# Layer 2 of a four-layer convolution kernel: who stores its sums, when squares are taken, and where raw strips are scaled

## Chip, core and metric

The kernel runs on one core of one Trainium2 chip, in float32 throughout. Times are microseconds (us) on the device. PE stands for TensorE's matmuls, PEld for its weight loads, DVE for VectorE, ACT for ScalarE, POOL for GpSimd and SP for SyncE, which here only issues DMAs. ScalarE and GpSimd have DMA queues of their own too, and issue from them in order with their other instructions.

## The reference

A tensor `x` of 4 images, 384 channels and 64x64 pixels goes through four layers, each of the form `x = x + layer(groupnorm(x))`: attention on 96 channels with a projection (layer 0), a patchwise Fourier filter with a gated depthwise convolution (layer 1), the block below (layer 2), and a 7x7 depthwise convolution whose kernels depend on the data (layer 3). The change lies in layer 2 and at the end of layer 1. Layer 2 begins so (`_bn` normalises each channel over the whole batch):

```python
kw = jax.nn.softmax(_bn(_pw(a, kp_w2), kp_g2, kp_b2), axis=1)
y3 = _bn(_dw(x, c3_w, 1), c3_g, c3_b)
y5 = _bn(_dw(x, c5_w, 2), c5_g, c5_b)
y1 = x * c1_w.reshape(1, -1, 1, 1) + c1_b.reshape(1, -1, 1, 1)
tok = _bn(kw[:, 0:1] * y3 + kw[:, 1:2] * y5 + y1, ar_g, ar_b)
```

`tok` is then gated and goes through a two-layer channel network. The statistics of `tok` over the batch (its sum and sum of squares by channel) are needed before that network can start.

## The kernel before

**End of layer 1.** `layer1` works on bands of eight image rows. `band_out` (L1142) multiplies a band's 512 pixels with the output weights, three output blocks `o` of 128 channels with two matmuls each, adds the block to `x` on VectorE, and stores the result to `x1`. For the last image it also calls `raw_strips` after the first block: four TensorE transposes of the first 128 channels, copied by ScalarE into `z`, the array of strips that layer 2's convolution reads. These strips are raw, since the group norm of the last image isn't known yet. The first blocks of the other images come normalised.

**Layer 2's first stage, `phase_b` (L1200).** It runs over twelve units of 32 channels for all four images. `strip_factors` makes scale and shift of the last image's strips by channel, spread over partitions (one matmul with `mean128`), and `scale_strips` applies them with a multiplication and an addition on VectorE, 32 channels at a time: the first quarter before the convolutions, the others in unit 0 after steps 3, 7 and 11.

A unit has sixteen steps `n`, one for a pair of channels. `matrices53` builds the banded matrix `toep` of a pair, by VectorE and GpSimd in turn (from the fifth on, odd ones by GpSimd), some three steps ahead; GpSimd's queue also loads the taps, once in four steps. `conv53` runs the 3x3 and 5x5 convolutions of the pair as matmuls into a PSUM bank `conv_m` (four banks), ScalarE copies it out to `d_o` in two copies, VectorE takes its statistics, and after each fourth step ScalarE's queue stores 1 MB to `d53`. When the unit's steps are done, `conv_norms` turns its statistics into coefficients `s` and `s0`.

**The sums of a unit, `unit_tok` (L1476).** A unit later, the results are read back in another layout, in four loads of 1 MB on SP's queue (`load_results`, pool `b_c` of three buffers), and combined with the normalised input in `unit_x`. Each quarter has two halves `h`: ScalarE writes the product of input and `c1_w` into a PSUM bank `tok_m` (one bank; for the last unit the four of `conv_m`), and two VectorE instructions add the two convolutions, the second writing over `unit_x` and summing up. After the second half ScalarE squares the quarter (writing into the spent `c_d`, for the sum of squares only), and SP's queue stores it to `tok`. It is a generator: each `yield` ends a piece, and `phase_b` takes a piece at even steps from 2 on and at step 15 (in the last unit after nearly every step).

**The strips of the next unit, `unit_strips` (L1301).** Loads of `unit_x` on SP's queue (two tiles of 2048 columns, eight DMAs each), norms on ScalarE by 1024 columns, and, from the fifth unit on, transposes on TensorE with copies by ScalarE and VectorE into `z`. A unit's strips begin at step 11 of the unit two before. The pool `b_x` has six tiles; a tile comes free when its two stores to `tok` have landed.

`units` turns the norm into the layout of units, and `nets` is the small network of `kw` and a gate, in three pieces taken at every third step. `tok_stats` ends the stage, and the channel network's matmuls (L1649) follow in `phase_ef`.

The framework orders instructions of each engine at build time by priority (mostly the order in the program) and by when it reckons that they are ready, and puts in the semaphores. So engines run their instructions in a fixed order, which need not be that of the text. PSUM has eight banks: four for `conv_m`, one for `band7_p`, two for small products, one for `tok_m`.

## Time and profile before

| what | us |
|---|---|
| median of three runs | 4839.67 (4834.68 to 4847.07) |
| profiled execution | 4846.3 |
| its span, first to last instruction | 4844.5 |
| first convolution of layer 2 starts | 2458.29 |
| last convolution of layer 2 ends | 3023.8 |
| first matmul of the channel network | 3069.84 |
| stores of `tok`, issued on SP | 48 of 0.34 |
| squares on ScalarE (L1501) | 48 of 1.15, and 0.19 to read the sum |
| products on ScalarE (L1489) | 96 of 0.78 |
| `scale_strips` on VectorE (L1183, L1184) | 8 of 1.95 to 2.05 |

The span is what the profile covers; the time of an execution is 1.8 us longer. A row of the waits names the waiting engine and line, what ended the wait, and the total, the number and the longest of such waits. The granted clock of TensorE was 0.951 of full speed in the mean.

### The profile page before, as it was taken

To read this page: it belongs to the slowest core of one execution; us is meant where nothing else is said; L and a number is where in the kernel's file an instruction comes from. 1 tells how busy PE (TensorE), PEld (TensorE's weight loads), DVE (VectorE), ACT (ScalarE), POOL (GpSimd) and SP (SyncE) were. 2 spreads that over 40 slices of the span, in tenths; PEclk is the share of its full clock that TensorE was granted. 3 is DMA by queue.
4 is the path that set the end of the run, shared out by engine and by line. 5 is a ranking of instruction groups with operands and counts; after the bars stand their busy time and mean duration, and the time that the engine had idled before them with its cause. 6 is when DMAs were issued, how large, how long until landed. Compare 5 with 4: busy or idle time off the path is not lost. (4 is left out here: it accounts for less than half of the span.)

```text
span 4844.5 us, 49738 instructions
## 1 busy us (share of the span) xinstructions
PE 4396.7 (91%) x18447; PEld 2451.9 (51%) x18447; DVE 2909.2 (60%) x4654; ACT 1994.1 (41%) x2976; POOL 757.3 (16%) x644
## 2 busy tenths in 40 slices
PE   7999999999999999989977988699999997778888
PEld 2233444344443444435466888344444443667888
DVE  6766555645656455556777777555521113767898
ACT  4444434444444444335345565221233334763321
POOL 1000000000000000000044555000000001235544
PEclk9999999999999999989988989899999998788999
DMA  4312211211112111123258888866654444895776
GB/s 141 104 38 68 74 53 66 73 52 46 65 60 68 40 59 59 52 73 109 72 157 283 299 295 299 282 258 252 239 232 152 156 156 156 325 342 181 231 256 232
DMA packets 289087, 745.55 MB, mean 154 GB/s; under 512 B 22491, under 2 KB 122950, under 8 KB 276806
## 3 DMA queue, kind: packets, MB, share of 16 engines
q1 hardware_dynamic: 226168, 452.52, 29.3%
q0 software_dynamic: 36624, 168.19, 9.2%
q10 hardware_dynamic: 26046, 121.58, 6.3%
q8 instruction: 149, 2.44, 0.2%
q14 instruction: 100, 0.82, 0.1%
HBM read 439.95 MB, written 302.25 MB: 153 GB/s over the span
## 5 line engine op out<-in xcount | busy, mean ns | idle before, releaser
L819 ACT ACTIVATE probs<-sc_s 128x1024 f32<-128x1024 f32 x512 | 496.5, 1019 | 689.2 <-PE av L929 588.2
L929 PE MATMUL av<-probs,vt 128*128 128x512 f32 x1536 | 715.0, 602 | 0.0
L1128 DVE SCALAR_TENSOR_TENSOR acc<-band,vecs,acc 128x512 f32<-128x512 f32 x708 | 494.0, 745 | 49.8 <-POOL band L1089 45.5
L1705 PE MATMUL h_m<-f_h,cm_w_t 128*128 128x512 f32 x1152 | 497.6, 596 | 7.4 <-ACT f_h L1693 7.4
L1411 PE MATMUL conv_m<-toep,z 128*128 128x192 f32 (+1 forms) x2304 | 446.9, 355 | 17.0 <-DVE z L1184 6.2
L929 PEld LDWEIGHTS av<-probs,vt 128*128 128x128 f32 x1536 | 276.3, 191 | 337.5 <-issue 333.8
L1411 PEld LDWEIGHTS conv_m<-toep,z 128*128 128x128 f32 x2304 | 409.0, 197 | 40.1 <-DVE z L1184 6.3
L2019 PE MATMUL conv_m<-toep,z 128*128 128x128 f32 x3072 | 393.7, 286 | 38.4 <-POOL toep L2006 16.9
L2019 PEld LDWEIGHTS conv_m<-toep,z 128*128 128x128 f32 x3072 | 379.7, 203 | 40.4 <-POOL toep L2006 17.3
L1649 PE MATMUL h_s<-e_tok,cm_w_t 128*128 128x512 f32 x768 | 363.1, 596 | 4.1 <-DVE e_tok L1634 4.1
L1705 PEld LDWEIGHTS h_m<-f_h,cm_w_t 128*128 128x128 f32 x1152 | 220.4, 191 | 284.6 <-issue 274.0
L1713 DVE BATCH_NORM_STATS2 h_st<-f_h 128x6 f32<-128x512 f32 x96 | 66.4, 694 | 430.1 <-ACT f_h L1712 430.1
L811 PE MATMUL sc_s<-q,k 32*128 32x512 f32 x2048 | 307.5, 642 | 15.4 <-ACT probs L819 15.2
L1392 POOL TENSOR_TENSOR toep<-w,band 128x1280 f32<-128x1280 f32 x94 | 276.1, 2938 | 240.3 <-PE conv_m L1411 234.8
L1051 PE MATMUL t_m<-w_in_t,xb 128*128 128x384 f32 x768 | 279.9, 500 | 4.7 <-DVE coef L1068 4.7
L965 PE MATMUL proj_m<-xm,w_proj_t 128*128 128x512 f32 x576 | 271.7, 611 | 6.3 <-DVE xm L904 4.9
L1656 ACT COPY e_h<-h_s 128x1024 f32<-128x1024 f32 x96 | 97.2, 1012 | 400.7 <-PE h_s L1649 400.7
L1658 DVE BATCH_NORM_STATS2 h_st<-e_h 128x6 f32<-128x512 f32 x192 | 123.5, 685 | 213.2 <-ACT e_h L1656 213.2
L1649 PEld LDWEIGHTS h_s<-e_tok,cm_w_t 128*128 128x128 f32 x768 | 147.1, 192 | 188.1 <-issue 183.4
L1051 PEld LDWEIGHTS t_m<-w_in_t,xb 128*128 128x128 f32 x768 | 143.2, 193 | 141.7 <-issue 56.1
L972 DVE SCALAR_TENSOR_TENSOR x_res<-proj_m,bn_c,x_res 128x512 f32<-128x512 f32 x96 | 71.7, 747 | 236.5 <-PE proj_m L965 236.3
L1649 PE MATMUL h_s<-z,cm_w_t 128*128 128x512 f32 x384 | 197.1, 595 | 0.0
(433 smaller groups left out, 6417.3 us busy)
## 6 DMA issues: line engine op xcount, KB each, us to landing
d<-d_o ACTq DMA_DIRECT2D x48, 1024.0 KB
c_d<-d SPq DMA_DIRECT2D x48, 1024.0 KB
hid<-e_h ACTq DMA_DIRECT2D x16, 3072.0 KB
f_h<-hid SPq DMA_DIRECT2D x16, 3072.0 KB
x_in<-in_x SPq DMA_DIRECT2D x96, 256.0 KB
x_res<-in_x SPq DMA_DIRECT2D x32, 768.0 KB
xa<-x_res POOLq DMA_DIRECT2D x32, 768.0 KB, 3.9
xa_out<-xa SPq DMA_DIRECT2D x32, 768.0 KB
```

Of the source, the lines that this page charges most:

```text
L811: nc.tensor.matmul(s[:, g], lhsT=k4[32 * g : 32 * g + 32, c], rhs=q[i][32 * g : 32 * g + 32], start=True, stop=True,)
L819: nc.scalar.activation(p[:, h * 1024 : (h + 1) * 1024], s[:, 2 * h : 2 * h + 2].rearrange("p a b -> p (a b)"), AF.Exp, scale=0.25,)
L929: nc.tensor.matmul(av[0], lhsT=vt[:, 4 * c + v, :], rhs=p[:, v * 512 : (v + 1) * 512], start=c == 0 and v == 0, stop=c == 7 and v == 3,)
L965: nc.tensor.matmul(m, lhsT=self.w_proj[:, j, o * P : (o + 1) * P], rhs=xm[:, j], start=j == 0, stop=j == NJ - 1,)
L1051: nc.tensor.matmul(m[:, 0:C], lhsT=xb[:, j], rhs=self.w_in[:, j, :], start=j == 0, stop=j == NJ - 1,)
L1128: nc.vector.scalar_tensor_tensor(out, src(j, k), w, done, ALU.mult, ALU.add)
L1392: eng.tensor_tensor(t, self.w53[:, at : at + 160].rearrange("p (m n) -> p m n", n=8).unsqueeze(2).to_broadcast([P, 20, 8, 8]), band.rearra ...
L1411: nc.tensor.matmul(m[:, c * 256 + to : c * 256 + to + 64 * (k1 - k0)], lhsT=self.z_[:, at : at + P], rhs=t[:, 10 * c + k0 : 10 * c + k1].r ...
L1649: nc.tensor.matmul(s[:, v, :], lhsT=w1[:, j, o * P : (o + 1) * P], rhs=t[j][:, v * 512 : (v + 1) * 512], start=j == 0, stop=j == NJ - 1,)
L1658: nc.vector.bn_stats(st[:, o, 8 * b + 2 * i + v, :], h[:, o, v * 512 : (v + 1) * 512])
L1705: nc.tensor.matmul(m, lhsT=w2[:, o, j * P : (j + 1) * P], rhs=h[:, o, v * 512 : (v + 1) * 512], start=o == 0, stop=o == 5,)
L2019: nc.tensor.matmul(m[:, ch * P : (ch + 1) * P], lhsT=self.z_[:, at : at + P], rhs=t[:, 8 * c + 2 * i : 8 * c + 2 * i + 2].rearrange("p m a ...
```

## The change

In `band_out` the raw strips of the last image are made after all three output blocks. `scale_strips` takes the first channel, a count and an engine: VectorE scales 8 channels after one matrix and 24 more after three, GpSimd scales the other three quarters, at the same steps as before. `units` and the set-up of `nets` move behind the first convolution. At step 0 of a unit three results of the unit before are asked for at once, and the fourth after the first quarter's square. Products have two banks of their own in all units, `conv_m` three. The square and the store of a quarter are made in the next piece, after that piece's product, and the store is issued by ScalarE; the last quarter's square and store of a unit come at step 0 of the unit after the next (`before`).

```diff
--- before.py
+++ after.py
@@ -1150,9 +1150,9 @@
                 m, lhsT=self.w_out[64:P, 1, o * P : (o + 1) * P], rhs=acc[2][64:P], start=False, stop=True
             )
             nc.vector.tensor_add(x[:, o], x[:, o], m)
-            if o == 0 and b == B - 1:
-                self.raw_strips(b, h, x[:, 0])
             yield 2.0
+        if b == B - 1:
+            self.raw_strips(b, h, x[:, 0])
         self.stats(st, x, h)
         nc.gpsimd.dma_start(self.x1[b][:, :, h * 512 : (h + 1) * 512], x)
 
@@ -1175,13 +1175,13 @@
         nc.tensor.matmul(m, lhsT=self.mean128, rhs=t.rearrange("p i c -> p (i c)"), start=True, stop=True)
         nc.vector.tensor_copy(self.z_rep, m.rearrange("p (i c) -> p i c", i=2))
 
-    def scale_strips(self, b, q):
-
-        at = slice(32 * q, 32 * q + 32)
+    def scale_strips(self, b, c0, n, eng):
+
+        at = slice(c0, c0 + n)
         zv = self.z[:, at, 1:33, b]
-        of = lambda i: self.z_rep[:, i, at].unsqueeze(2).to_broadcast([P, 32, 32])
-        self.nc.vector.tensor_mul(zv, zv, of(0))
-        self.nc.vector.tensor_add(zv, zv, of(1))
+        of = lambda i: self.z_rep[:, i, at].unsqueeze(2).to_broadcast([P, n, 32])
+        eng.tensor_mul(zv, zv, of(0))
+        eng.tensor_add(zv, zv, of(1))
 
     def coef(self, name):
         return self.keep.tile([P, NJ, B], F32, tag=name, name=name)
@@ -1216,27 +1216,34 @@
             nc.gpsimd.memset(self.mean128, 1.0 / P)
             self.toep = {}
             for n in range(LEAD + 2):
-                if n == 2:
+                if n == 1:
                     self.strip_factors(B - 1)
-                    self.scale_strips(B - 1, 0)
+                    self.scale_strips(B - 1, 0, 8, nc.vector)
+                if n == 3:
+                    self.scale_strips(B - 1, 8, 24, nc.vector)
                 self.matrices53(n)
-            self.units(cp)
             self.unit_x = [[] for _ in range(UNITS)]
             first, strips, behind = self.unit_strips(0), self.unit_strips(1), None
-            for _ in range(3):
-                next(first)
+            next(first)
             for u in range(UNITS):
                 st = self.bt_p.tile([P, 2, 16, 6], F32, tag="st", name="st")
                 tok = self.unit_tok(u - 1) if u else first
-                nets = iter(()) if u else self.nets(cp)
                 for n in range(16):
                     if u or n > 1:
                         self.matrices53(16 * u + n + LEAD)
                     self.conv53(u, n, st)
+                    if n == 0 and not u:
+                        self.units(cp)
+                        nets = self.nets(cp)
+                        for _ in range(2):
+                            next(first)
+                    if n == 0 and u > 1:
+                        next(before, None)
                     if n == 0 and u:
+                        self.results = [self.load_results(u - 1, i) for i in range(3)]
                         self.conv_norms(u - 1, behind)
                     if not u and n in (3, 7, 11):
-                        self.scale_strips(B - 1, n // 4 + 1)
+                        self.scale_strips(B - 1, 8 * n + 8, 32, nc.gpsimd)
                     if n % 2:
                         next(strips, None)
                     elif n or not u:
@@ -1256,10 +1263,10 @@
                         next(coming)
                         if n == 15:
                             strips = coming
-                behind = st
-            results = [self.load_results(UNITS - 1, i, self.bx_p, "x") for i in range(4)]
+                behind, before = st, tok
+            self.results = [self.load_results(UNITS - 1, i, self.bx_p, "x") for i in range(4)]
             self.conv_norms(UNITS - 1, behind)
-            for _ in self.unit_tok(UNITS - 1, results):
+            for _ in self.unit_tok(UNITS - 1):
                 pass
             self.tok_stats()
         self.taps_s.close()
@@ -1404,7 +1411,7 @@
         t = self.toep.pop(16 * u + n)
         if n % 4 == 0:
             self.d_o = self.bt_p.tile([P, 8, 2, P], F32, tag="d_o", name="d_o")
-        m = self.psum.tile([P, 512], F32, tag="c", name="conv_m", bufs=4)
+        m = self.psum.tile([P, 512], F32, tag="c", name="conv_m", bufs=3)
         for c in range(2):
             for i, k0, k1, to in ((1, 3, 7, 0), (0, 0, 3, 0), (2, 7, 10, 64)):
                 at = (c0 + c) * 132 + 4 * i
@@ -1465,7 +1472,8 @@
         nc.vector.scalar_tensor_tensor(s0, m[:, 7:8], -1.0, s0, ALU.mult, ALU.add)
         self.tok_s = s, s0
 
-    def load_results(self, u, i, pool, tag):
+    def load_results(self, u, i, pool=None, tag="d"):
+        pool = pool or self.bc_p
         d = pool.tile([P, 2 * 8 * P], F32, tag=tag, name="c_d").rearrange("p (y v n) -> p y v n", v=2, n=P)
         self.nc.sync.dma_start(
             d.rearrange("p y v n -> p y (v n)"),
@@ -1473,22 +1481,25 @@
         )
         return d
 
-    def unit_tok(self, u, results=None):
-
-        nc = self.nc
-        j, q = u // 4, u % 4
+    def unit_tok(self, u):
+
+        nc = self.nc
         s, s0 = self.tok_s
+        results, self.results = self.results, None
+        behind = None
         for i in range(4):
-            sl = slice(i * 1024, (i + 1) * 1024)
-            d = results[i] if results else self.load_results(u, i, self.bc_p, "d")
+            d = results[i]
             o = self.unit_x[u][i // 2][:, i % 2 * 1024 : i % 2 * 1024 + 1024]
             for h in range(2):
                 part = slice(h * 512, (h + 1) * 512)
-                last = u == UNITS - 1
-                m = self.psum.tile([P, 512], F32, tag="c" if last else "t", name="tok_m", bufs=4 if last else 1)
+                m = self.psum.tile([P, 512], F32, tag="t", name="tok_m", bufs=2)
                 nc.scalar.activation(
                     m, o[:, part], AF.Identity, bias=s0, scale=self.vec("c1_w")[:, u : u + 1]
                 )
+                if h == 0 and behind is not None:
+                    self.square_and_store(u, *behind)
+                    if len(results) == 3:
+                        results.append(self.load_results(u, 3))
                 mv, ov = (t.rearrange("p (y n) -> p y n", n=P) for t in (m, o[:, part]))
                 of = lambda v: d[:, 4 * h : 4 * h + 4, v]
                 nc.vector.scalar_tensor_tensor(mv, of(1), s[:, 1:2], mv, ALU.mult, ALU.add)
@@ -1496,17 +1507,21 @@
                 nc.vector.scalar_tensor_tensor(
                     ov, of(0), s[:, 0:1], mv, ALU.mult, ALU.add, accum_out=self.total[:, u, k : k + 1]
                 )
-                if h == 0:
-                    yield
-            nc.scalar.activation(
-                d.rearrange("p y v n -> p (y v n)")[:, 0:1024],
-                o,
-                AF.Square,
-                bias=self.about[:, u : u + 1],
-                accum_out=self.squares[:, u, i : i + 1],
-            )
-            nc.sync.dma_start(self.tok[u, :, :, sl].rearrange("b c n -> (b c) n"), o)
-            yield
+                yield
+            behind = i, d, o
+        self.square_and_store(u, *behind)
+
+    def square_and_store(self, u, i, d, o):
+
+        nc = self.nc
+        nc.scalar.activation(
+            d.rearrange("p y v n -> p (y v n)")[:, 0:1024],
+            o,
+            AF.Square,
+            bias=self.about[:, u : u + 1],
+            accum_out=self.squares[:, u, i : i + 1],
+        )
+        nc.scalar.dma_start(self.tok[u, :, :, i * 1024 : i * 1024 + 1024].rearrange("b c n -> (b c) n"), o)
 
     def tok_stats(self):
 
```

## The prediction

> **What bounds the kernel now.** I read the page first, for the stage that the change touches. The engine row says that TensorE is busy nine tenths of the span, and the slices say where it is not: the changed code runs from about 2430 to 3070 us, slices 20 to 25.
>
> ```profile
> PE 4396.7 (91%) x18447; PEld 2451.9 (51%) x18447; DVE 2909.2 (60%) x4654; ACT 1994.1 (41%) x2976; POOL 757.3 (16%) x644
> ...
> PE   7999999999999999989977988699999997778888
> ...
> PEclk9999999999999999989988989899999998788999
> ```
>
> The 7, 7 and 6 among nines are layer 2's convolution stage. Next I cut it at the matmuls of `conv_norms` (L1443), which come once a unit, and asked for busy times in these stretches: unit 0, units 2, 3, 8, 9 and 10, and the tail up to the first matmul of the next stage.
>
> ```profile
> 2458.30:2507.60 49.30, 42.51 (x210) 38.94 (x210) 44.67 (x79) 27.07 (x56) 30.80 (x13) 0.90 0.41 135
> ...
> 2548.00:2584.60 36.60, 36.29 (x204) 34.37 (x204) 34.27 (x72) 23.91 (x56) 25.35 (x13) 1.00 0.89 305
> 2584.60:2654.30 69.70, 38.70 (x211) 35.49 (x211) 43.68 (x88) 38.83 (x76) 23.17 (x12) 0.77 0.83 275
> ...
> 2843.00:2889.30 46.30, 39.39 (x223) 36.66 (x221) 35.85 (x74) 29.36 (x63) 25.58 (x12) 0.91 0.93 319
> 2889.30:2935.30 46.00, 44.18 (x246) 41.62 (x247) 36.34 (x74) 27.94 (x61) 25.57 (x12) 0.94 0.88 284
> 2935.30:2984.50 49.20, 39.45 (x224) 36.73 (x223) 36.75 (x75) 29.45 (x63) 25.57 (x12) 0.88 0.94 323
> ...
> 3024.00:3069.80 45.80, 5.04 (x24) 4.13 (x24) 24.07 (x84) 21.45 (x40) 0.58 (x1) 0.54 0.90 301
> ```
>
> Columns are the stretch, its length, busy PE, PEld, DVE, ACT and POOL, clock, DMA share and GB/s. The reader is to see a stage that reaches TensorE's pace once (unit 2) and loses 6 to 10 us a unit later and 30 us in unit 3, while DMA is nearly full all the time. What ends the idle time stands in the waits from 2480 to 3026 us (total, times, longest):
>
> ```profile
> PEld strip_m L1335 <- ACT unit_x L1320: 58.0, 12, 22.5
> ACT tok_m L1489 <- DVE unit_x L1496: 54.7, 33, 5.6
> ACT c_d L1501 <- DVE unit_x L1496: 23.1, 25, 2.7
> ```
>
> TensorE waits for ScalarE's norm of the next strips; ScalarE is held in order by products that wait for their one bank and squares that wait for VectorE. The norms need loads, so the last view is the waits of the SP queue, 2440 to 3060 us:
>
> ```profile
> SPq L1312 <- DMA d<-d_o: 125.1, 17, 33.1
> SPq L1508 <- DVE st L1425: 101.3, 18, 15.9
> SPq L1312 <- DMA tok<-unit_x: 56.2, 18, 6.4
> SPq L1508 <- DVE unit_x L1496: 48.7, 11, 17.2
> ```
>
> Stores of sums (L1508) stand in SP's queue until VectorE is done (180 us with the smaller rows), with loads behind them. The timeline shows the stage's start, and the chain of waits its tail:
>
> ```profile
> 2456.28 1.96 DVE L1184 TENSOR_TENSOR z<-z,z_rep 128x1024 f32<-128x1024 f32 x1
> ...
> 2458.29 12.47 PE L1411 MATMUL conv_m<-toep,z 128*128 128x256 f32 x60 [6.22 <-DVE z L1184]
> ```
> ```profile
> 3030.86 10.59 DMA tok<-unit_x
> 3041.48 0.05 issue
> 3041.59 8.38 DMA c_d<-d
> ```
>
> **What the Trainium skill says.** *SBUF — State Buffer*, "Who interferes with whom": a VectorE instruction with two SBUF inputs contends with a GpSimd one that reads SBUF, and the later one blocks fully. The trace agrees: a 12x1 product (L385) took 2.10 us and a GpSimd matrix 5.61 instead of 2.9 us while both engines worked on SBUF. *DMA: Bandwidth & Descriptors*, "Issuing engines are not separate DMA queues": the queues of SP and ScalarE end on the same 16 engines, so a second issuer saves only issuing time. Total rate staying at 275 to 325 GB/s with two queues at work doesn't contradict it, and I credit no bandwidth. *TensorE: Matmul & The Clock Gate*, Part 1: an idle array drops to half clock and needs some us of work to come back. Here the twelve matmuls of a pair of channels take 2.2 us in steady running and 4.5 us after a stall, so each stall costs about 2 us more than its length, and strips 1 us more.
>
> **The change part by part**, from the profiled execution's 4846.3 us (span 4844.5, 1.8 around it), which is 6.6 above the median of 4839.7.
>
> *Raw strips behind the outputs.* For the last image's eight bands the four transposes no longer make TensorE wait for VectorE's add between outputs. At the last band the second output's matmul stood at 2436.76 behind transposes from 2435.77; it comes 1 us earlier, and with it the norm. Bands before have TensorE at 19 of 20 us; nothing is taken for them. −1 us, between 0 and −3.
>
> *First scale in 8 channels, fewer matrices ahead.* The norm is known at 2445.7, the first convolution starts at 2458.3: 12.6 us with five matrices (1.44 to 1.48 each), factors, and two passes of 1.96 us on VectorE. Afterwards what must precede it is one matrix 1.4, factors 0.5, their matmul 1.2, copy 0.4, and two passes over 256 instead of 1024 elements, about 0.5 each: 4.5 to 5 us with waits between. That is −7.5, and the 24 further channels (two passes of about 1.5) lie beside the first four pairs at about 2.5 us each. Bounds −4 to −9.
>
> *Three scalings on GpSimd.* Six passes of 1.97 us (11.8) leave VectorE in unit 0, where ScalarE waited 8.08 us for the nets' L385 and TensorE 4.94 us behind it. GpSimd pays. Price: its matrices take 2.9 us for 1280 elements, so 2.3 for 1024; *GPSIMD Engine Reference*, 3.1, gives 4497 ns for 2048, the same. Six are 13.9 us on 30.8 busy in unit 0's 49.3: nearly full, and the tap loads in GpSimd's queue come up to 4.6 us later, covered by the three matrices of lead (6.5 us). The nets' small products can still be locked out for 2.3 us each. −3 us, between −8 and +6.
>
> *Stores on ScalarE's queue.* 48 issues of 0.34 us leave SP; SP's loads stand behind no store. ScalarE pays 1.4 us a unit, of 40 where it is busy 24 to 29: no cost by itself. Each store now waits for its square (1.33 us later than before), which frees `unit_x` for loads later by that. Behind a store on ScalarE stand the evacuations of `conv_m`, and TensorE behind them.
>
> *Two banks for products, squares a piece later, three results at once.* The 77.8 us of ScalarE waiting on VectorE go where a bank is free and the square's data old. In unit 3's catch-up (2630 to 2652) a block of two halves takes 5.98 us in lockstep; VectorE's four passes and reads alone are 3.1 and ScalarE's three steps 2.9. Four blocks in the stall save about 11 us if the lag stays. The lag arose since unit 0's results were asked for only at 2532.3, 25 us after its last convolution, behind sixteen strip loads; asked for first, the stall of 22.13+5.13+2.52 us could go whole. I take −18, between −8 and −28. For the boundaries of units 4 to 10 the idle times before strips, norms and the next convolution add to 34.5 us in the timeline, with slow clock about 50. What is late next is the load of the second half tile, now behind three results of 1 MB: at some 300 GB/s, 3.5 us each, plus 9 us until the last `d` has landed, it comes about 22 us into a unit of 40. Its norm belongs at the seventh pair (15 us). So a third: −17, between −40 and +20.
>
> *Banks of `conv_m` 4 to 3.* TensorE's run-ahead falls from 8.7 to 6.5 us. The longest string of other work on ScalarE is product 0.78, square 1.33, issue 0.34, norm 1.24, two strip copies 1.2: 4.9 us. Nominally free; +5 for pile-ups, between 0 and +20.
>
> *Tail.* Results 3 and 4 waited for unit 10's last store, which stood on SP behind result 1 and landed after 10.59 us beside result 2. On ScalarE's queue it leaves 1 to 2 us earlier and in its own ring. −4, between 0 and −8. Two banks instead of four cost nothing, VectorE (1.5 us a half) sets the pace.
>
> Sum: −1 −7.5 −3 −18 −17 +5 −4 = −45.5: 4801 for an execution like the profiled one, 4794 for the median; I say 4795.
>
> **Rivals.** *DMA is the bound.* For it: share 0.83 to 0.94 in every unit and unchanged bytes. Against it: unit 2 ran at TensorE's pace with 0.89, and 2843 to 2858 us has gaps. Then only the start, the lockstep saving and the tail stay, −20: 4820. *ScalarE's queue blocks (slower).* SP's loads waited 125 us for completions of `d` stores that they don't read, so a DMA is held until an older one of either queue is done. If one of the eight stores a unit that ScalarE now issues is held so, behind loads that wait for buffers, all evacuations stand. It decides from 6.5 us, three banks. The wait at 2962.85 was 10.82 us: 4.3 lost plus 2 for the clock, and the norm behind it as late, say 8 a unit, eleven units: +88; the gains at boundaries and half of unit 3's go (17+9), leaving −20: about +68 at full strength, half the units +24; I put it at 4870. Against it: ScalarE's 48 `d` stores show no such wait longer than 0.8 us. *It doesn't take effect*: the instruction order may hoist loads as before; then 4836.
>
> **How the numbers follow.** Forecast 0.48 (its own range 4765 to 4825), DMA bound 0.24 (a quarter of it within the bound), blocked queue 0.26, no effect 0.02. A measurement of this kernel can tell about 0.3%, 14.5 us. Faster 0.48+0.18 = 0.66, same 0.06+0.02 = 0.08, slower 0.26. The range reaches down to 4750 (all boundary stalls and unit 3's gone) and up to 4868, leaving out about half of the slower case and a few per cent below.
>
> **What would show it.** Right: the first convolution about 5 us after the last image's norm, where it is 12.6 now; unit 3 below 55 us; ScalarE's waits for `unit_x` from VectorE under 25 us; results asked for within 10 us of a unit's last convolution. Wrong: ScalarE idle before `d_o` or a store with DMA as releaser, matmuls waiting for `d_o`, GpSimd's matrices ending waits of TensorE in unit 0, or strips still waiting for `unit_x` loads for more than 30 us.

## The result, and the profile after

The changed kernel takes 4795.86 us (median of four runs, 4790.60 to 4806.85) where the kernel before took 4840.60 beside it: a ratio of 0.991, with a 95% interval of 0.9888 to 0.9932. The forecast was 4795. That the sum came out is half luck, though. Several terms missed, in opposite directions, and the table below says where the time went.

First the page of the changed kernel, the same rows as before: busy times, and the slices of the span.

```profile
PE 4391.7 (92%) x18447; PEld 2441.5 (51%) x18447; DVE 2902.5 (61%) x4650; ACT 1992.9 (42%) x2976; POOL 771.0 (16%) x650
...
PE   7999999999999999989978998799999996778888
...
PEclk9999999999999999999989999899999998788999
```

Over the whole span busy times hardly moved (GpSimd has 14 us more), while the span fell from 4844.5 to 4796.5 us. The stage alone looks different. From the last image's norm to the channel network TensorE's idle time fell from 126.0 to 89.3 us, and its busy time from 498.2 to 483.0 for the same 2710 matmuls, with a granted clock of 0.93 in the mean, 0.87 before. Units 4 to 10 show it best, before and after (columns: stretch, length, busy PE, PEld, DVE, ACT and POOL, clock, DMA share, GB/s):

```profile
2654.30:2984.50 330.20, 295.64 (x1638) 276.57 (x1639) 251.73 (x507) 198.22 (x430) 178.95 (x84) 0.92 0.89 297
2653.60:2945.80 292.20, 277.95 (x1639) 261.09 (x1638) 252.16 (x512) 199.05 (x434) 178.75 (x85) 1.00 0.98 332
```

Of the 38 us, 20.3 are idle time and 17.7 are busy time that a full clock shortened. (Before the norm TensorE was busy 9.1 us longer in the second profile, so that the sums over the span are alike.) The stretches below are again cut at the matmuls of `cn_rep` (now L1450): units 0, 1 and 3, a steady unit (8), and the tail.

```profile
2468.78:2517.91 49.13, 43.28 (x213) 39.95 (x213) 41.67 (x76) 26.91 (x57) 36.69 (x17) 0.90 0.49 166
2517.91:2564.10 46.19, 42.97 (x215) 40.41 (x216) 33.77 (x69) 25.62 (x55) 25.23 (x13) 0.89 0.84 288
2607.00:2653.60 46.60, 40.19 (x223) 37.36 (x224) 36.61 (x74) 29.47 (x65) 23.15 (x12) 0.93 0.92 309
2820.40:2862.08 41.68, 39.69 (x235) 37.30 (x235) 35.98 (x74) 28.66 (x63) 25.56 (x13) 1.00 0.98 333
2981.40:3027.20 45.80, 4.68 (x25) 3.72 (x24) 24.11 (x81) 19.52 (x36) 0.59 (x1) 0.56 0.97 315
```

The reader is to see unit 8: TensorE busy 39.7 of 41.7 us at full clock, at the highest DMA rate of any stretch here. Every unit from the fourth to the tenth now takes 41.7 to 42.0 us, where before they took 44.4 to 50.1. Unit 3 went from 69.7 to 46.6. Unit 1 grew from 40.3 to 46.2, and the tail stayed.

The waits from the start of unit 0 to the last convolution (2480 to 2984 us; total, times, longest):

```profile
ACT unit_x L1327 <- DMA unit_x<-x: 27.1, 12, 8.2
...
ACT c_d L1517 <- DVE unit_x L1507: 19.2, 18, 3.2
...
ACT tok_m L1496 <- DVE unit_x L1507: 6.0, 5, 3.7
```
```profile
PEld conv_m L1418 <- ACT d_o L1429: 15.7, 9, 2.1
...
PEld strip_m L1342 <- ACT unit_x L1327: 4.7, 1, 4.7
```

ScalarE's product no longer waits for VectorE (54.7 before, 6.0 now), and TensorE no longer waits for the strips' norm (58.0, now 4.7). New is the 15.7 us that the weight loads put down to a `conv_m` bank, 4.1 before. In seven of the nine cases, just before a unit's end, the matmul itself names VectorE's copy of the next strips into `z` (L1347), which ended 0.4 us after the bank came free in the one I followed (2817.26 and 2816.85 us). ScalarE waits for input loads 27.1 us, where it was 6.2; that reaches TensorE only once.

**One thing has to be taken out before stages are compared.** The last image's norm (L1028) became known at 2445.67 us in the profile before and at 2454.95 here, and in the twelve further kernels anywhere from 2436.7 to 2453.6. Layer 1 differs among them only in the place of the raw strips, so most of this is drift between executions. The fair measure of the stage is from that norm to the first matmul of the channel network:

| us | before | after | forecast | measured |
|---|---|---|---|---|
| last band's first output matmul to norm | 15.8 | 17.9 | −1 | +2.1 |
| norm to first convolution | 12.6 | 13.8 | −7.5 | +1.2 |
| unit 0 | 49.3 | 49.1 | −3 and +5 | −0.2 |
| units 1 to 3 | 146.6 | 135.7 | −18 | −10.9 |
| units 4 to 10 | 330.3 | 292.2 | −17 | −38.0 |
| unit 11 | 39.2 | 35.6 | none | −3.6 |
| tail | 46.1 | 45.8 | −4 | −0.3 |
| norm to channel network | 624.2 | 572.3 | | −51.9 |

The rows add up to −49.7, beside −45.5 forecast. (What follows the stage took 5.4 us less in the second profile and wasn't touched. What precedes the last band took 7.1 more; there the edit reaches the last image's seven other bands, and it saves 0.7 us in the last two of them, as the section on the raw strips shows.) The last row of a single profile is good to about 5 us: two variants below differ by 5 there and not in time.

### The profile page after: what moved, and what is told of

It is laid out like the page before. It is cut to its first block, busy times and chain, and to the rows that moved or that the text cites. A ratio compares the mean times of both kernels' runs of the same rounds, so it can differ in the third digit from the quotient of the medians.

```text
span 4796.5 us, 49708 instructions
## 1 busy us (share of the span) xinstructions
PE 4391.7 (92%) x18447; PEld 2441.5 (51%) x18447; DVE 2902.5 (61%) x4650; ACT 1992.9 (42%) x2976; POOL 771.0 (16%) x650
## 3 DMA queue, kind: packets, MB, share of 16 engines
q8 instruction: 149, 2.44, 0.2%
## 5 line engine op out<-in xcount | busy, mean ns | idle before, releaser
L1418 PEld LDWEIGHTS conv_m<-toep,z 128*128 128x128 f32 x2304 | 403.6, 195 | 54.2 <-ACT d_o L1429 15.7
```

The source lines that it names most:

```text
L1418: nc.tensor.matmul(m[:, c * 256 + to : c * 256 + to + 64 * (k1 - k0)], lhsT=self.z_[:, at : at + P], rhs=t[:, 10 * c + k0 : 10 * c + k1].r ...
```

## The experiments

All times are medians; ratios are to the kernel before on the same chip. "Stage" is the last row of the table above.

### The start: who scales, and when (e1_scale_dve, e2_scale_behind)

The timeline of the changed kernel's start, by GpSimd, VectorE and TensorE, shows why the first convolution came later rather than earlier:

```profile
2459.72 5.03 POOL L1183 TENSOR_TENSOR z<-z,z_rep 128x1024 f32<-128x1024 f32 x2 [8.86 <-DVE z_rep L1176]
2464.70 6.18 POOL L1184 TENSOR_TENSOR z<-z,z_rep 128x1024 f32<-128x1024 f32 x2
```
```profile
2460.89 5.22 DVE L1183 TENSOR_TENSOR z<-z,z_rep 128x256 f32<-128x256 f32 x2
2465.96 6.33 DVE L1184 TENSOR_TENSOR z<-z,z_rep 128x256 f32<-128x256 f32 x2
```
```profile
2468.78 1.54 PE L1418 MATMUL conv_m<-toep,z 128*128 128x256 f32 x3 [8.84 <-DVE z L1184]
```

GpSimd's scalings stand in the program after steps 3, 7 and 11. Beyond the raw strips they depend on nothing but `z_rep`, and the framework put them at the head of GpSimd's order. So they ran beside VectorE's scalings for the first pairs. (A row of the timeline that joins two instructions shows the shape of the first: each of VectorE's rows is the pass over 8 channels and the pass over 24.) Two kernels take this apart. The first gives the three scalings back to VectorE:

```diff
-                        self.scale_strips(B - 1, 8 * n + 8, 32, nc.gpsimd)
+                        self.scale_strips(B - 1, 8 * n + 8, 32, nc.vector)
```

> The changed kernel with the three later scalings on VectorE instead of GpSimd. In the changed kernel the first convolution starts 13.9 us after the last image's norm is known (2468.8 against 2454.9), where about 5 were forecast. Theory (GpSimd's passes over z were ordered ahead of VectorE's two small ones and hold the shared SBUF port): VectorE's small passes take about 0.5 us each instead of 2.6 to 3.2, the first convolution comes 5 to 7 us after the norm, unit 0 becomes some us longer, and the whole time falls by 2 to 8 us. Rival (the chain of factors, their matmul and the copy is itself so long): the first convolution stays 12 us or more after the norm, and the time doesn't fall.

The second leaves them on GpSimd but orders them behind its matrices:

```diff
-        eng.tensor_mul(zv, zv, of(0))
-        eng.tensor_add(zv, zv, of(1))
+        behind = self.tc.issue_after(self.pool_toep.ins) if eng is self.nc.gpsimd else nullcontext()
+        with behind:
+            eng.tensor_mul(zv, zv, of(0))
+            eng.tensor_add(zv, zv, of(1))
...
+        if eng is nc.gpsimd:
+            self.pool_toep = made
```

> The changed kernel with each GpSimd scaling ordered behind GpSimd's latest matrix. Theory (shared port at the start): first convolution 5 to 7 us after the norm, unit 0 no longer than 49 us up to the first statistics matmul, time about 8 us below the changed kernel (4788). Rival (GpSimd is then too full in unit 0, its matrices come late): TensorE waits for GpSimd's matrices in unit 0 and the gain is given back, time unchanged within 4 us.

VectorE's part of the timeline with GpSimd ordered behind:

```profile
2454.48 2.02 DVE L1185 TENSOR_TENSOR z<-z,z_rep 128x256 f32<-128x256 f32 x2
2456.41 2.04 DVE L1186 TENSOR_TENSOR z<-z,z_rep 128x256 f32<-128x256 f32 x2
```

The same four passes take 4.06 us alone and 11.55 beside GpSimd. That fits the lock of the Trainium skill's *SBUF — State Buffer*, "Who interferes with whom", which the prediction named for the small products of unit 0 and not for the place where it hit. In both kernels the first convolution comes 8.5 us after the norm, not 13.8. It isn't 5, since in the framework's order three matrices and the multiplication of the other 24 channels still stand ahead of it.

Neither kernel is clearly faster, however: 4792.08 us (0.9897, 0.9877 to 0.9917) and 4791.96 (0.9898, 0.9880 to 0.9916). Unit 0 grew to 55.2 and 55.1 us, so that from the norm to the end of unit 0 it took 63.8 and 63.7, with 63.0 in the changed kernel and 62.0 before. So the start's gain is given back within unit 0. With GpSimd ordered behind, TensorE waits there 7.4 us for the unit's last statistics and 2.9 us for a bank, and none of its waits is ended by a GpSimd matrix, which the rival had expected. I read this as a scaling that has to be paid beside unit 0's matrices and nets by one engine or the other; which instruction costs the time isn't shown.

### The raw strips (e7_raw_old)

```diff
+            if o == 0 and b == B - 1:
+                self.raw_strips(b, h, x[:, 0])
             yield 2.0
-        if b == B - 1:
-            self.raw_strips(b, h, x[:, 0])
```

> The changed kernel with the raw strips made after the first output block, as before. The last image's norm is known 17.9 us after the last band's first output matmul in the changed kernel, 15.8 us before the change. Theory A (moving the strips made the end of layer 1 longer, since the array stayed at low clock): 15.8 again, and time 2 us less. Theory B (the clock's state at that place is chance): the length depends on when TensorE comes to full clock, not on the strips' place; 15 to 18 us, time unchanged within 4 us.

The old place gives 4787.47 us (0.9888, 0.9869 to 0.9908), 8 below the changed kernel in separate comparisons. The intervals of the two overlap, and the stage is 571.7 us, the same. What differs in the traces is the end of layer 1. TensorE's timeline of the last band, changed kernel first, then with the old place:

```profile
2441.04 2.07 PE L1148 MATMUL out_m<-acc,w_out_t 128*128 128x512 f32 x2
2443.04 2.07 PE L1149 MATMUL out_m<-acc,w_out_t 64*128 64x512 f32 x2
2445.04 2.07 PE L1148 MATMUL out_m<-acc,w_out_t 128*128 128x512 f32 x2
2447.05 2.07 PE L1149 MATMUL out_m<-acc,w_out_t 64*128 64x512 f32 x2
```
```profile
2442.16 1.06 PE L1164 MATMUL strip_m<-ident,xa_out 128*128 128x128 f32 x4
2443.15 1.16 PE L1149 MATMUL out_m<-acc,w_out_t 64*128 64x512 f32 x2
2444.24 1.12 PE L1148 MATMUL out_m<-acc,w_out_t 128*128 128x512 f32 x2
2445.29 1.12 PE L1149 MATMUL out_m<-acc,w_out_t 64*128 64x512 f32 x2
```

With the transposes in between, the last three pairs of matmuls run at full clock (1.12 to 1.16 us); without them the pairs stay at 2.07. From the first output matmul to the norm it is 17.9 us in all eight kernels of this study that have the transposes last, every pair at 2.07. Of the six that have them in between, five take 15.7 or 15.8 us, with the clock up; in the sixth (e11 below) the clock stays down and it is 18.8. So the transposes cost 0.9 us, as forecast, and what they mostly bring with them, the clock, gives 3.0 back. Why the clock comes up behind them, the records don't say.

The two bands before go the other way. From one band's first output matmul to the next, the last three intervals take 22.1, 24.1 and 20.0 us in all kernels with the old place and 22.1, 23.7 and 19.7 in all with the new one. So the new place costs 2.1 us in the last band, saves 0.7 before it, and makes the end of layer 1 about 1.5 us longer. The rest of the 8 us is in no stretch that I could find; it lies within the drift of the norm.

### The stores' queue (e3_store_sp), and the stores alone (e11_b_store_act)

```diff
-        nc.scalar.dma_start(self.tok[u, :, :, i * 1024 : i * 1024 + 1024].rearrange("b c n -> (b c) n"), o)
+        nc.sync.dma_start(self.tok[u, :, :, i * 1024 : i * 1024 + 1024].rearrange("b c n -> (b c) n"), o)
```

> The changed kernel with the stores of tok issued by SP again. The units 4 to 10 take 41.7 to 42.0 us in the changed kernel, 44 to 50 before. Theory A (loads stood behind stores on SP): these units go back to 44 us or more, strips wait for norms again, time +15 to +30 us. Theory B (asking for the results at once and the delayed squares did it, the issuer is nearly free): units stay below 42.5 us, time within 5 us.

Measured 4822.06 us (0.9959, 0.9944 to 0.9975): 26 us of the 45 are gone, units 4 to 10 take 323.1 us. The waits of that kernel's SP and PEld (2440 to 2990 us) show the old pattern back:

```profile
SPq L1478 <- DMA d<-d_o: 159.9, 17, 13.8
...
SPq L1524 <- DVE st L1432: 29.2, 19, 7.2
```
```profile
PEld strip_m L1342 <- ACT unit_x L1327: 33.6, 13, 9.7
```

The store stands on SP until VectorE has its sums, loads stand behind it, and TensorE waits for strips again. Results suffer too, though the program asks for them at once: in units 4 to 9 the second and third are issued 10 to 24 us after a unit's end, where the changed kernel needs 3 to 6. The first row above is their waiting; in the changed kernel it is 80.5 us. The counterpart is the kernel before with only this edit, on `sl` in `unit_tok` (L1508):

```diff
-            nc.sync.dma_start(self.tok[u, :, :, sl].rearrange("b c n -> (b c) n"), o)
+            nc.scalar.dma_start(self.tok[u, :, :, sl].rearrange("b c n -> (b c) n"), o)
```

> Before with only the stores of sums issued by ScalarE. Results asked for at once alone gave 22.7 us of the 45; both, undone singly from after, cost 26 and 21. Theory A (each takes its own waits off SP's queue, and they add): about 4815 to 4820 us, and the SP waits for st and unit_x gone. Theory B (either alone removes most of what a full SP queue costs, the other is then worth less): about 4800. Theory C (without results asked for early the stores' place is worth nothing): within 5 us of before, units 4 to 10 still 46 to 50.

4840.49 us, 1.0005 (0.9996 to 1.0014): nothing. Theory C held. Its waits, for PE, ACT and SP, 2440 to 2990 us:

```profile
PE cn_rep L1443 <- DVE st L1425: 40.8, 9, 6.1
```
```profile
ACT tok_m L1489 <- DVE unit_x L1496: 38.5, 29, 4.2
ACT c_d L1501 <- DVE unit_x L1496: 35.2, 31, 1.9
```
```profile
SPq L1470 <- ACT c_d L1501: 60.6, 9, 14.2
```

No store waits on SP any more, and strips wait 21.6 us instead of 58. In exchange results, still asked for one by one, wait for the squares that free their buffers; the products lie late in the unit, in lockstep over one bank; and VectorE's statistics stand behind them, so that TensorE waits up to 6.1 us at each unit's end. Units 6 to 10 take 47.5 to 47.8 us each. The stall changed its place.

### The results (e6_load_late), and the results alone (e8_b_load_early)

```diff
-                        self.results = [self.load_results(u - 1, i) for i in range(3)]
+                        self.results = None
...
-            d = results[i]
+            d = results[i] if results else self.load_results(u, i)
...
-                    if len(results) == 3:
-                        results.append(self.load_results(u, 3))
```

> The changed kernel with each quarter's result asked for in its own piece, as before. Theory A (results asked for late made the sums lag and the strips' loads late): unit 3 goes back over 55 us, units 4 to 10 over 43.5, time +20 to +40. Theory B (the framework puts loads ahead anyway, the stores' queue did it): time within 5 us.

4817.39 us (0.9950, 0.9931 to 0.9969): 21.5 us back, with unit 3 at 51.7 (theory A said over 55) and units 4 to 10 at 312.5. The kernel before with results asked for as the changed one does (three at step 0, the fourth after the first quarter's square):

```diff
                     if n == 0 and u:
+                        self.results = [self.load_results(u - 1, i, self.bc_p, "d") for i in range(3)]
                         self.conv_norms(u - 1, behind)
...
-            d = results[i] if results else self.load_results(u, i, self.bc_p, "d")
+            d = results[i]
...
+            if len(results) == 3:
+                results.append(self.load_results(u, 3, self.bc_p, "d"))
```

> The kernel before, with only the results of a unit asked for at once at step 0 (three, and the fourth after the first quarter), stores still on SP, one bank, squares at once. Theory A (late results are the cause of unit 3's 30 us): unit 3 falls below 50 us and the time by 20 us or more. Theory B (stores on SP's queue hold the loads whatever the order): unit 3 stays over 60 us, time within 8 us of the kernel before.

4815.18 us (0.9952, 0.9933 to 0.9971), 22.6 us less than before. Unit 3 fell from 69.7 to 56.6 us, not below 50 as theory A had it, and units 4 to 10 add up to 329.4, no better than before, and irregular (40.4 to 52.5). So this edit alone shortens the catch-up and does nothing for the later units. Its waits of SP show what holds the later units:

```profile
SPq L1471 <- DMA d<-d_o: 110.5, 14, 10.9
SPq L1511 <- DVE st L1426: 51.0, 16, 8.2
```

### Banks (e4_one_bank), and squares (e5_square_now)

```diff
-        m = self.psum.tile([P, 512], F32, tag="c", name="conv_m", bufs=3)
+        m = self.psum.tile([P, 512], F32, tag="c", name="conv_m", bufs=4)
...
-                m = self.psum.tile([P, 512], F32, tag="t", name="tok_m", bufs=2)
+                m = self.psum.tile([P, 512], F32, tag="t", name="tok_m", bufs=1)
```

> The changed kernel with one bank for products and four for convolutions, as before. Theory A (lockstep of ScalarE and VectorE held the norms): ScalarE's waits for unit_x from VectorE go back from 25 to over 50 us, units 4 to 10 become 1 to 4 us longer each, time +10 to +25. Theory B (with the squares a piece later the product's bank is free in time anyway; three banks for convolutions cost some waits): time within 5 us of the changed kernel, or a few us below it, and TensorE's waits for d_o (15.7 us) shrink.

4816.55 us (0.9950, 0.9933 to 0.9967). ScalarE's wait for the one product bank is back (2480 to 2984 us; 6.0 in the changed kernel), as theory A said:

```profile
ACT tok_m L1496 <- DVE unit_x L1507: 127.9, 63, 5.1
```

Its units 0 and 1, a steady unit and the tail:

```profile
2464.29:2508.03 43.74, 41.76 (x216) 38.21 (x216) 40.50 (x76) 26.39 (x57) 35.90 (x17) 0.95 0.50 162
2508.00:2546.40 38.40, 38.37 (x216) 36.59 (x217) 29.37 (x61) 20.31 (x46) 26.54 (x13) 1.00 0.87 285
2773.22:2817.65 44.43, 41.69 (x236) 38.61 (x236) 36.31 (x73) 28.00 (x62) 25.59 (x13) 0.96 0.92 316
2984.10:3043.40 59.30, 5.72 (x25) 4.73 (x24) 29.78 (x95) 24.59 (x46) 0.58 (x1) 0.53 0.90 295
```

The edit trades one bank for the other, so only unit 0, which has no products, shows the convolutions' bank alone: taking it costs 5.4 us. From unit 1 on the figures are net. The trade costs 7.8 us in unit 1, of which unit 2 returns 4.6 (42.9 in the changed kernel, 47.5 here), and it brings 2.7 us in each steady unit, 18.8 in units 4 to 10, and 13.5 in the tail, where one bank here stands against the four that the kernel before used there. TensorE's waits for a `conv_m` bank don't go with the fourth bank: they are 15.1 us here and 15.7 in the changed kernel.

Squares at once instead of a piece later:

```diff
-                if h == 0 and behind is not None:
-                    self.square_and_store(u, *behind)
-                    if len(results) == 3:
-                        results.append(self.load_results(u, 3))
-                yield
-            behind = i, d, o
-        self.square_and_store(u, *behind)
+                if h == 0:
+                    yield
+            self.square_and_store(u, i, d, o)
+            if len(results) == 3:
+                results.append(self.load_results(u, 3))
+            yield
```

> The changed kernel with square and store made right after a quarter's second half, as before. Theory A (squares that wait for VectorE hold ScalarE, and with it norms and copies): ScalarE's wait for c_d from unit_x rises well over 19 us, units 4 to 10 grow by 1 to 4 us, time +10 to +25. Theory B (only the order of DMAs matters): units within 0.5 us of 41.7, time within 5 us, perhaps a little less since stores leave a piece sooner.

4800.70 us (0.9908, 0.9876 to 0.9941), not to be told from the changed kernel's 0.9910; units 4 to 10 add up to 293.8. With two banks, delaying the square is worth nothing that can be measured.

### One ring of five banks (e9_shared, e10_shared_raw)

Units 0 and 1 want banks for convolutions, later units for products. A common ring seemed to serve both:

```diff
-        m = self.psum.tile([P, 512], F32, tag="c", name="conv_m", bufs=3)
+        m = self.psum.tile([P, 512], F32, tag="c", name="conv_m", bufs=5)
...
-                m = self.psum.tile([P, 512], F32, tag="t", name="tok_m", bufs=2)
+                m = self.psum.tile([P, 512], F32, tag="c", name="tok_m", bufs=5)
```

> After with products and convolutions in one ring of five PSUM banks instead of two and three. Theory A (what matters in units 0 and 1 is how many banks convolutions have, later how many products have): units 0 and 1 lose 5 us each or more against after (49.1 and 46.2), the steady units stay within 0.5 us of 41.7, the tail at 46; about 4785 us. Theory B (in one ring a product that waits for VectorE holds the bank that the next convolution is due to get, so the split matters more than the number): steady units of 43 us or more, about 4805 us or more.

> The ring of five banks, and the raw strips back behind the first output of a band. If the two savings add (the transposes' place is worth about 2 us at the last band and independent of the banks): 2 us less than the ring alone, last band's first output matmul to norm about 15.8 us where it is 17.9 in after. If the single comparison of the raw strips before (8 us less) was more than the 2 us that its stage shows: 5 to 8 us less than the ring alone.

4836.71 us (0.9993, 0.9983 to 1.0004): all of the gain is lost. Unit 0 came down to 43.7 us as hoped, but unit 1 only to 45.3, units 4 to 10 take 328.5 and unit 11 takes 53.0. One of them:

```profile
2823.61:2872.00 48.39, 43.70 (x234) 40.23 (x234) 36.88 (x74) 28.75 (x63) 25.54 (x12) 0.93 0.88 290
```

That is theory B's size, but its mechanism isn't shown: the framework also ordered the queues anew, so that statistics and transposes stand at other places between the convolutions (TensorE waits 2.4 us for `st` at this unit's end), and the two effects can't be parted here. With the raw strips back (e10) it is 4832.05 us (0.9983, 0.9973 to 0.9992), 4.7 less, with overlapping intervals. The traces show 2.2 us of it in the last band (15.7 to 17.9), about 1.5 with the bands before, and the same stage (614.9 and 615.3 us). That the place is worth more than this isn't shown.

### Five banks in unit 0 only (e13_five_raw)

Unit 0 has no products, so their two banks are free there. With the raw strips in the old place:

```diff
-        m = self.psum.tile([P, 512], F32, tag="c", name="conv_m", bufs=3)
+        m = self.psum.tile([P, 512], F32, tag="ct"[x := not u and n % 5 > 2], name="conv_m", bufs=3 - x)
```

> After with the raw strips back behind the first output of a band, and with the two product banks, which hold nothing before unit 1, given to two of every five convolution pairs of unit 0. Theory A (unit 0 of after waits on three convolution banks; four banks gave it 43.7 us and a ring of five 43.7, three give 49.1): unit 0 about 44 us, the steady units unchanged at 41.7, 5 us less than the version with the raw strips back alone, about 4782 us. Theory B (what unit 0 gains is lost in units 1 and 2, which then wait for the same loads): unit 0 about 44 us, units 1 and 2 together 4 us or more longer than their 89, about 4787 us.

4782.63 us (0.9880, 0.9859 to 0.9901), the fastest of the study, with unit 0 and unit 5:

```profile
2462.38:2506.31 43.93, 42.51 (x221) 39.41 (x221) 40.58 (x77) 26.47 (x57) 36.66 (x17) 0.94 0.46 152
2720.03:2762.18 42.15, 39.96 (x236) 37.27 (x235) 36.17 (x74) 28.39 (x63) 25.54 (x13) 1.00 0.96 332
```

Unit 0 lost 5.1 us against the kernel with the raw strips alone (49.0), units 1 and 2 together take 86.6 where they took 88.8 there: theory A. The step of 4.8 us from that kernel was measured in separate comparisons, whose intervals overlap; the 44 us of unit 0 carry it.

## Why the prediction was right, and where it was not

**Right in the mechanism.** The gain comes from ScalarE's lockstep with VectorE and from loads that stood behind stores, in unit 3 and at the boundaries. Two of the four signs it named showed: unit 3 took 46.6 us (it said below 55), and from unit 1 on the three results are asked for 2 to 6 us after a unit's end (it said within 10); of unit 0's only the first is, the others come 15.6, 16.0 and 34.3 us after. A third was on the line: ScalarE waits 25.2 us for `unit_x` from VectorE (it said under 25). The fourth failed, the first convolution. Of the signs of being wrong, TensorE did wait for `conv_m` banks, and a GpSimd matrix ended one wait of it, 3.5 us, but in unit 1.

**The start (−7.5 forecast, +1.2 measured)** is the step that failed. It priced VectorE's passes as if alone, while the change gave GpSimd passes over the same array that depend on nothing later. The text had weighed the lock only for unit 0's small products. The lock cost 5.3 us, the difference to e1 and e2. Without it the first convolution would have come 4 of the 7.5 us earlier; the other 3.5 fail since the prediction counted one matrix ahead of it, and the framework put three there.

**The three scalings on GpSimd (−3)** did help within unit 0, by more: 49.1 us where e1, with the same banks, takes 55.2. But their early passes held up the start, and from the norm to the end of unit 0 the difference is 0.8 us (63.0 and 63.8). **The banks (+5)** cost 5.4 us in unit 0 (43.7 in e4, 49.1) and about 9 net in units 0 to 3 (175.6 in e4, 184.8), which is within its bounds and nearly twice its size.

**Units 1 to 3 (−18 for unit 3, −10.9 measured).** Unit 3 itself gave 23.1 us, but units 1 and 2 took 12.2 back. A unit's sums have eight products. Before, ScalarE made 2, 8 and 13 of them during units 1, 2 and 3; now it makes eight in each, beside convolutions that have a bank fewer. The prediction counted the catch-up's end and not the place that its work would go to.

**The boundaries of units 4 to 10 (−17 forecast, −38.0 measured)** are the term that was mis-sized, and it made good for the others. The text took a third of some 50 us of idle time and slow clock, and 38 went, 20.3 of idle time and 17.7 of slow clock. It took so little since the second half tile's load would land some 22 us into a unit and its norm belonged at the seventh pair. The load did come so: in the unit from 2820.40 its first norm ran at 2840.57, 20.2 us in. But the norm didn't belong earlier. In the changed kernel's fixed order the transposes that read it stand at 2844.86, behind 24.5 us of other matmuls. In units 5 to 8 a norm now ends 2.3 to 10.7 us before its transposes start (0.1 us in one case), where before it was 0.1 to 3.0. TensorE stood still for a late strip only once in the stage.

**What the parts do together** is what the list of separate terms hid. Units 4 to 10:

| results at once | stores on ScalarE | two product banks | units 4 to 10, us | kernel |
|---|---|---|---|---|
| | | | 330.3 | before |
| yes | | | 329.4 | e8 |
| | yes | | 333.8 | e11 |
| yes | | yes | 323.1 | e3 |
| | yes | yes | 312.5 | e6 |
| yes | yes | | 311.0 | e4 |
| yes | yes | yes | 292.2 | after |

Each of these two alone brings nothing here, pairs bring 7 to 19 us, all three 38. The six kernels of this study that have all three take 292.2 to 296.1, so a single profile is good to about 4 us here. The rows differ in more than the three columns: e8 and e11 have the other parts of the kernel before, squares at once among them, and the rest those of the changed kernel; e5 says that the squares' place is worth nothing with two banks. My reading is that a late result, a late input and a full product bank each hold the same in-order engines, and that what is left over sets the pace; the table shows that they don't add, not how. (The two product banks alone weren't tried.)

**The tail (−4, −0.3 measured).** The stores no longer precede the loads of results, but the last results are late all the same. From its chain of waits:

```profile
2991.26 13.92 DMA c_d<-d
...
3010.25 9.10 DMA tok<-unit_x
3019.37 3.17 DMA e_tok<-tok
```

The last result is asked for 8.6 us after the unit's end (15.3 before) and takes 13.92 us (8.38 before), beside three others and, from 2995 us on, the loads of `e_tok`. So what the queue gave, the transfer took back. Whether two product banks instead of four cost something in the tail wasn't tested.

**The raw strips (−1, +2.1 measured, about +1.5 with the bands before).** The text saw the wait that the transposes cause, 0.9 us by e11, and not that the clock mostly comes up behind them.

**The rivals.** *DMA is the bound* would have left units 4 to 10 as they were; the steady unit refutes it, at 333 GB/s where unit 8 had 319 before. A share near 0.9 did not mean that there was no room. Whether transfers are the next bound, at 0.98, wasn't tested. *ScalarE's queue blocks* had its point at a store held longer than 6.5 us. The trace shows no wait of ScalarE before `d_o` that a DMA ended, the longest issue of a store on its queue is 1.34 us, and the waits of TensorE put down to a bank add to 15.7 us, none longer than 2.1. One detail of the prediction was wrong here: a store doesn't wait for its square. It is issued just before or beside it (2838.61 and 2838.66 us).

## What to carry to other kernels

Where one in-order queue holds several late things, undo each part singly from the full change as well as adding it alone: here the stores' queue was worth 0 us alone and 26 in company. When work is moved to an engine that another one can lock out, look at what it depends on and not where it stands in the text: here the framework started it as soon as that was ready. Buffers can serve two uses in different phases (banks lent in unit 0), but pooling them for good moved the order of everything else.

## What the runs showed of the hardware

- Four scaling passes of VectorE took 4.06 us alone and 11.55 beside GpSimd's passes over the same array. GpSimd's pairs took 5.03 and 6.18 meanwhile, where the last pass, beside none of VectorE's, took 2.44, so 4.9 for a pair. VectorE lost 7.5 us.
- Twelve output matmuls in a row stayed at 2.07 us a pair over 12 us (granted clock 0.50), after a gap of 7.4 us, in eight kernels of eight; with four transposes between them the pairs behind ran in 1.12 to 1.34 in five of six. The Trainium skill's *TensorE: Matmul & The Clock Gate*, Part 1, lets some 3.4 us of sustained work bring the clock up; these runs differ.
- A DMA share near 0.9 was no ceiling: units 4 to 10 had 0.89 and 297 GB/s in the mean before and 0.98 and 332 GB/s after.
- In units 4 to 10 the clock was 0.92 with stalls and 1.00 without, and TensorE's busy time for the same matmuls 295.6 and 278.0 us: 17.7 us of 38 came from the clock.
